# Two seams of a product stage: the place of its buffers, the last store of spectra and the first loads after it

## The chip, the cores and the metric

The kernel runs on one core of one Trainium2 chip as one launch. The metric is the device time of a run in microseconds (us). A run of the kernel is also recorded by the hardware profiler once; that execution has a time of its own and a span, from its first to its last instruction.

## The reference

Input is an image batch `x` of 16 x 128 channels x 32 x 32 (float32). Two layers follow, each with a mixing part and a token part, both with a residual. Cut to what matters:

```python
# layer 0
x = x + _L0_conv_ref(_ln_c(x), ...)        # linear attention
t = _to_tokens(x)                          # (16, 1024, 128)
t = t + _L0_ffn_ref(_ln_t(t), ...)         # spectral filters, see below
x = _from_tokens(t, x)
# layer 1
x = x + _L1_conv_ref(_ln_c(x), ...)        # two 3x3 convolutions
t = _to_tokens(x)
t = t + _L1_ffn_ref(_ln_t(t), ...)         # experts that choose tokens
x = _from_tokens(t, x)
```

The spectral part convolves every token sequence with 16 filters `phi`, once as it is and once with alternating signs, and multiplies the results with matrices `M_phi_plus` and `M_phi_minus`:

```python
U_plus = irfft(Vf[None, :, :, None] * Uf_p[:, :, None, :], n=n, axis=1)[:, :sl]
out = einsum('btkd,k,kde->bte', U_plus, s, Mpp) + einsum('btkd,k,kde->bte', U_minus, s, Mpm)
```

In the frequency domain this is one 128 x 128 complex matrix for each frequency, multiplied with the spectra of all 16 samples.

## The kernel before

The kernel has three stages, one after the other.

**Stage A** (to about 387 us) goes over the 16 samples in a software pipeline: attention, normalisation, and at last the spectrum `xf` of each sample. A dictionary of steps, `period`, gives the order. The last steps of a sample are `taps_add` (L633: a sum on VectorE, and the store of the sample to DRAM, `xd`, L634) and `odd_turns4` (L614: the last butterflies on POOL, and the store of the sample's spectrum to DRAM, `vd`, L615, 1 MB). `vd` has 16 chunks of frequencies as its first dimension. `prepare` stores weights for later (`wid`, L722).

**The product stage** (to about 664 us) goes over the 16 chunks `c`.
- `begin(c)` loads the chunk's spectra of all samples in four parts of four samples (`xc`, L778, issued on SP), and POOL makes sums and differences of each part (two L781 and one L782 each) into the tile `v`.
- `generate(c, q)` lets TensorE build a chunk's matrices from filters and `M_phi` (L790) in PSUM; `collect` copies them into the matrix buffer `g` (L801 on VectorE, L803 on ScalarE). There are two buffers `g`, for even and odd chunks, and the matrices of chunk `c + 1` are made between the products of chunk `c`.
- `multiply(c, m, x, ...)` makes the products of group `m` of four (L814). ScalarE copies them out of PSUM into one tile `yt` (L875), `combine` adds and subtracts its halves into the result tile `ys` (L842, L843, VectorE), and after the fourth group `finish` does four more sums (L828 to L831; on POOL, and on VectorE for the last chunk) and stores the results to DRAM, `yd`, in two parts (L835). `yd` consists of one tensor for chunks 0 to 13 and one for chunks 14 and 15.

TensorE's order at the start is: `generate` of chunk 0, eight more tiles of `generate` of chunk 1, then the first products.

**The last stage** loads, for each sample `b`, its tokens (`xt[b]` from `xd`, L974) and results (`yts[b]` from the two tensors of `yd`, L977), transforms back (`even`, `odd_sd`, `inverse`; L990 on POOL, L1003 on VectorE, L1074 on TensorE), adds (L1081), and goes through convolutions and experts. `planned` computes the order of its steps from fixed costs and due times; `load` is called for samples 0 and 1 ahead of all steps, for the others in the order. There are two buffers `y`, so the third sample's load waits for the first sample's back transform. In `load`, sample 0's tokens and the large parts of the results of samples 0 and 1 are issued on POOL, the rest on SP.

**Order and memory.** In a block with `manual_schedule` the named engines keep the order in which the program is written; instructions of different blocks can be mixed. SP is among the named engines in the last stage only. Each tile pool takes a stretch of every partition's memory, one after the other in the order of opening. A pool opened where others were closed reuses their bytes, and its first accesses wait for all accesses to every pool that lies under it, not only for the tiles under them: in the program, the first L781 waits for the last stores of `xd`, `vd` and `wid`. Addresses in bytes of a partition:

| Pools | Stage A | Product stage | Last stage |
|---|---|---|---|
| constants, weights | 18,976 to 68,640 | lower part as before | 18,784 to 95,232 (`wi`, `cw`, convolution tiles, two `y`) |
| working tiles | 68,640 to 167,552 | | 160,768 to 227,936 |
| `spool`: two `xf` | 167,552 to 183,936 | | |
| `xpool`: eight `x` | 183,936 to 216,704 | | 95,232 to 99,328 (`x0`), 99,328 to 160,768 (`x1` to `x15`) |
| `ppool`: staging of `prepare` | 216,704 to 227,456 | | |
| `gpl0`, `gpl1`: even and odd `g` | | 43,552 to 109,088, 109,088 to 174,624 | |
| `cpl`: two `v`, two `ys`, `yt`, `ye` | | 174,624 to 219,680 | |
| `xcl`: four `xc` | | 219,680 to 227,872 | |

Of the kernel before, what the change touches and what calls it, by code (L numbers as in the profile page):

```python
# [8 lines left out]
F32 = mybir.dt.float32  # L9
# [60 lines left out]
def metaformer_kernel(ctx: ExitStack, tc: tile.TileContext, io: dict, out: bass.AP):  # L70
# [96 lines left out]
    with ExitStack() as l0:  # L167
# [43 lines left out]
        with ExitStack() as a0:  # L211
# [132 lines left out]
            class Attention:  # L344
# [267 lines left out]

                def odd_turns4(self):
                    butterflies(self.ao, self.xf, 1, self.sd)  # L614
                    nc.sync.dma_start(  # L615
                        vd[:, :, self.b, :].rearrange("c p w -> p c w"),
                        self.xf.rearrange("p c x r m j -> p c (x r m j)"),
                    )

                def taps(self):  # L620

# [138 lines left out]


        with ExitStack() as g0:
            gpl = [g0.enter_context(tc.tile_pool(name=f"gpl{i}", bufs=1)) for i in range(2)]
            cpl = g0.enter_context(tc.tile_pool(name="cpl", bufs=2))
            xcl = g0.enter_context(tc.tile_pool(name="xcl", bufs=1))
            psg = g0.enter_context(tc.tile_pool(name="psg", bufs=8, space=PSUM))
            gs, vs = {}, {}
# [71 lines left out]

            def combine(c, m, ys, t):  # L840

                nc.vector.tensor_tensor(ys[:, :, 0, m], t[:, 1], t[:, 0], ALU.add)  # L842
                nc.vector.scalar_tensor_tensor(  # L843
                    ys[:, :, 1, m], t[:, 1], -1.0, t[:, 0], ALU.mult, ALU.add
                )
                if m == NM - 1:
                    finish(c, ys)

            with tc.manual_schedule(engines=PINNED):
# [5 lines left out]
                for c in range(NCH):  # L855
                    if c + 1 < NCH:
                        gs[c + 1] = gpl[(c + 1) % 2].tile([P, CW, C], F32, name="g", tag="g")

                    ys = cpl.tile([P, JL // RG, 2, NM, C], F32, name="ys", tag="ys")
                    for m in range(NM):  # L860
                        if c + 1 < NCH:
                            pg = [generate(c + 1, 2 * m + x) for x in range(2)]
                            collect(c + 1, 2 * m, pg[0])
                        if waiting:
                            combine(*waiting)
                        if c + 1 < NCH:
                            if m == 0:
                                begin(c + 1)
                            collect(c + 1, 2 * m + 1, pg[1])
                        py = psg.tile([P, 2, JL // RG, C], F32, name="py", tag="p")  # L870
                        fresh = set()
                        for x in range(2):
                            multiply(c, m, x, py, fresh)
                        t = cpl.tile([P, 2, JL // RG, C], F32, name="yt", tag="yt", bufs=1)
                        nc.scalar.copy(t, py)  # L875
                        waiting = c, m, ys, t
                combine(*waiting)


# [11 lines left out]
    with ExitStack() as c1:  # L891

        cconst = c1.enter_context(tc.tile_pool(name="cconst", bufs=1))
        first = c1.enter_context(tc.tile_pool(name="cfirst", bufs=1))
        xpool = [c1.enter_context(tc.tile_pool(name=f"xpool{i}", bufs=1)) for i in (2, 3)]
        work = c1.enter_context(tc.tile_pool(name="cwork", bufs=2))
        cps = c1.enter_context(ExitStack())
        ps = cps.enter_context(tc.tile_pool(name="cps", bufs=2, space=PSUM))
# [71 lines left out]
        yts = {}  # L970

        def load(b):
            xt[b] = xpool[b > 0].tile([P, N], F32, name=f"x{b}", tag=f"x{b}")
            (nc.sync if b else nc.gpsimd).dma_start(xt[b], xd[b])  # L974
            yts[b] = first.tile([P, 2, 2 * NM, C], F32, name="y", tag="y", bufs=2)
            for i, js in enumerate((slice(P - 2 * JL), slice(P - 2 * JL, P))):
                (nc.gpsimd if b < 2 and i == 0 else nc.sync).dma_start(  # L977
                    yts[b][js].rearrange("p r x e -> p r (x e)"),
                    yd[i][:, :, b].rearrange("j r x e -> j r (x e)"),
                )  # L980
# [758 lines left out]
```

## Time and profile before

| | |
|---|---|
| Runs | median 1273.64 us of three (1272.99 to 1274.5) |
| Profiled execution | 1271.01 us, span 1269.2 us |
| Busy, share of the span | PE 1149.1 us (91%), VectorE (DVE) 936.2 (74%), ScalarE (ACT) 725.9 (57%), POOL 605.3 (48%) |
| Mean granted TensorE clock | 0.967 of full speed |
| DRAM traffic | 164.64 MB, mean 130 GB/s |

The page cuts the span into 40 slices, and a digit is the busy share of one in tenths. The timeline has one row for a run of like instructions: start, duration, engine, line, operation, what is written and read, how many, and in brackets how long the engine was idle ahead of it and what ended that. SPq and POOLq are the engines' own queues, where loads and stores are issued; "to landing" is the time from there until the data is in place. A matmul of float32 gives two records. A chain of waits follows the work that ended last back from step to step.

### The profile page before, as it was taken

How to read it: one execution, taken by the hardware profiler on the slowest of the kernel's cores; microseconds unless marked ns; L12 is line 12 of the kernel's file. 1: busy time of each engine (PE TensorE's matmuls, PEld its weight loads, DVE VectorE, ACT ScalarE, POOL GpSimd, SP SyncE). 2: the span in 40 equal slices, each digit the busy share in tenths (PEclk: the TensorE clock that was granted, in tenths of full speed). 3: DMA queues.
4: the chain of work that ended last, by engine and by line, in shares of the span. 5: the costliest groups of instructions: out<-in, count | busy, mean ns of one | idle time of the engine just before them, and what ended most of it. 6: DMA issues, size and time to landing. Idle time of an engine off the chain costs nothing. (4 is left out here: it accounts for less than half of the span.)

```text
span 1269.2 us, 34025 instructions
## 1 busy us (share of the span) xinstructions
PE 1149.1 (91%) x14244; PEld 934.4 (74%) x14244; DVE 936.2 (74%) x1944; ACT 725.9 (57%) x1420; POOL 605.3 (48%) x801
## 2 busy tenths in 40 slices
PE   4889999999997999999976999999999999977975
PEld 3677777777776998888865888888898888853432
DVE  5788888888765777776765798889898888772325
ACT  4777777767654777777742354565565556542111
POOL 2335545565666688888863444333353442210002
PEclk9999999999998999999998999999999999985998
DMA  7105343443345244444458231213222212055976
GB/s 264 33 30 165 117 139 124 134 158 111 106 134 183 87 136 137 137 136 136 130 196 244 72 81 34 83 34 84 67 55 77 70 50 101 27 190 190 389 285 265
DMA packets 88346, 164.64 MB, mean 130 GB/s; under 512 B 5632, under 2 KB 41728, under 8 KB 87552
## 3 DMA queue, kind: packets, MB, share of 16 engines
q1 hardware_dynamic: 87312, 159.05, 38.6%
q0 software_dynamic: 880, 3.41, 0.8%
q8 instruction: 112, 1.84, 0.6%
q14 instruction: 42, 0.34, 0.1%
HBM read 105.03 MB, written 57.41 MB: 128 GB/s over the span
## 5 line engine op out<-in xcount | busy, mean ns | idle before, releaser
L958 PE MATMUL pcv<-v,cw 128*128 128x256 f32 x1152 | 259.7, 381 | 0.7 <-POOL v L1144 0.7
L958 PEld LDWEIGHTS pcv<-v,cw 128*128 128x128 f32 x1152 | 215.9, 191 | 34.3 <-issue 4.9
L801 DVE COPY g<-pg 128x512 f32<-128x512 f32 x196 | 127.8, 682 | 77.1 <-PE pg L790 77.1
L803 ACT COPY g<-pg 128x512 f32<-128x512 f32 x316 | 161.2, 605 | 31.7 <-PE pg L790 30.9
L790 PE MATMUL pg<-ph,mst 32*128 32x128 f32 x4096 | 139.6, 278 | 5.0 <-issue 3.5
L790 PEld LDWEIGHTS pg<-ph,mst 32*128 32x128 f32 x4096 | 126.0, 186 | 19.1 <-issue 12.4
L814 PE MATMUL py<-g,v 128*32 128x128 f32 x4096 | 127.9, 276 | 8.5 <-POOL v L781 5.7
L814 PEld LDWEIGHTS py<-g,v 128*32 128x32 f32 x4096 | 110.1, 111 | 18.3 <-POOL v L781 5.8
L144 ACT ACTIVATE tok<-tok,sts 128x128 f32<-128x128 f32 x256 | 101.9, 480 | 16.8 <-DVE sts L1031 13.4
L135 DVE BATCH_NORM_STATS2 bst<-big 128x6 f32<-128x256 f32 x256 | 91.1, 416 | 23.3 <-PE big L152 14.1
L781 POOL TENSOR_TENSOR v<-xc 128x256 f32<-128x256 f32 x128 | 99.8, 803 | 8.9 <-DMA xd<-x 8.9
L626 PE MATMUL big<-u,mu 128*128 128x128 f32 (+4 forms) x384 | 86.0, 380 | 0.0
L1144 POOL TENSOR_TENSOR v<-abss 128x256 f32<-128x256 f32 x64 | 49.1, 788 | 66.1 <-DVE abss L1140 54.3
L277 POOL TENSOR_TENSOR xf<-ab 128x256 f32<-128x256 f32 x34 | 24.8, 729 | 112.3 <-DVE ab L244 112.3
L1163 POOL TENSOR_TENSOR yo<-abss 128x256 f32<-128x256 f32 x32 | 23.5, 736 | 109.1 <-DVE abss L1159 109.1
L626 PEld LDWEIGHTS big<-u,mu 128*128 128x128 f32 x384 | 56.7, 191 | 18.0 <-issue 15.4
L875 ACT COPY yt<-py 128x512 f32<-128x512 f32 x64 | 37.5, 586 | 48.9 <-PE py L814 26.4
L1580 POOL TENSOR_TENSOR x<-yt,x 128x1024 f32<-128x1024 f32 x4 | 9.4, 2359 | 115.2 <-ACT yt L1579 115.2
L559 PE MATMUL big<-wf,ub 128*128 128x256 f32 x256 | 62.0, 385 | 0.2
L144 ACT ACTIVATE tt<-tt,sts 128x128 f32<-128x128 f32 x128 | 51.1, 481 | 14.6 <-DVE sts L1031 14.6
L152 PEld LDWEIGHTS big<-ident,x 128*128 128x128 f32 x384 | 46.0, 146 | 17.7 <-issue 10.5
L782 POOL TENSOR_SCALAR v<-v 128x256 f32<-128x256 f32 x64 | 55.2, 862 | 5.6
(247 smaller groups left out, 2480.5 us busy)
## 6 DMA issues: line engine op xcount, KB each, us to landing
we<-in_weight SPq DMA_DIRECT2D x32, 1024.0 KB, 9.9
vd<-xf SPq DMA_DIRECT2D x16, 1024.0 KB, 5.1
xc<-vd SPq DMA_DIRECT2D x64, 256.0 KB, 3.2
yd<-ys SPq DMA_DIRECT2D x32, 512.0 KB, 4.0
y<-yd SPq DMA_DIRECT2D x14, 896.0 KB, 6.7
x<-in_x SPq DMA_DIRECT2D x16, 512.0 KB, 4.6
mi<-in_M_phi SPq DMA_DIRECT2D x16, 512.0 KB, 4.7
xd<-x SPq DMA_DIRECT2D x16, 512.0 KB, 6.1
```

The source lines that it names most:

```text
L135: nc.vector.bn_stats(bst[:, j : j + 2, :].rearrange("p j s -> p (j s)"), src[:, j : j + 2, :].rearrange("p j c -> p c j"),)
L144: nc.scalar.activation(dst[:, j, :], src[:, j, :], AF.Identity, bias=nm[:, j : j + 1], scale=r[:, j : j + 1],)
L559: nc.tensor.matmul(dst, self.ub[:, q, :], wf[:, q, :], start=True, stop=True)
L626: nc.tensor.matmul(self.pa[:, a:hi], mu[:, NF - 1 - si, tap, :], self.u[:, a - tap : hi - tap], start=(tap == 0), stop=(tap == KU - 1),)
L781: nc.gpsimd.tensor_tensor(vv[:, x, 1:, bs], e, o, op)
L782: nc.gpsimd.tensor_scalar(v[:, :, 0, bs], v[:, :, 2, bs], -1.0, None, ALU.mult)
L790: nc.tensor.matmul(pg[r][:, i], mst[rs, 4 * q + i, :], ph[rs, c, :], start=True, stop=True,)
L801: nc.vector.tensor_copy(dst, src)
L803: nc.scalar.copy(dst, src)
L814: nc.tensor.matmul(py[rows, x, kl, :], v[:, (x * NM + m) * JL + jl, 1 - ri : 3 - ri, :] .rearrange("p k b -> p (k b)"), g[:, ((x * 2 + ri) ...
L958: nc.tensor.matmul(pc[:, i], wt[:, dy, k, :], v[:, k, dy * WT : dy * WT + HT], start=(dy == 0), stop=(dy == 2),)
L1144: nc.gpsimd.tensor_tensor(v[:, k, WT : WT + HT], self.ab[:, 0], self.ab[:, 1], op)
```

## The change

- `cpl` is opened between the two matrix buffers. `v`, results and sums then lie at 109,088 to 154,144, the odd buffer at 154,144 to 219,680; all else keeps its place.
- The spectrum of the last sample is stored in two pieces: chunk 0 (64 KB), then the other fifteen.
- For the last chunk, ScalarE copies only the first half of the products, into two halves of `yt` in turn, and VectorE reads the second half from PSUM.
- `x0` lies in one pool with the other samples, 95,232 to 160,768.
- The large part of sample 1's results is loaded from SP's queue, in its place in the program (after `x1`), not from POOL's.

```diff
                 def odd_turns4(self):
                     butterflies(self.ao, self.xf, 1, self.sd)
-                    nc.sync.dma_start(
-                        vd[:, :, self.b, :].rearrange("c p w -> p c w"),
-                        self.xf.rearrange("p c x r m j -> p c (x r m j)"),
-                    )
+                    for cs in (slice(0, 1), slice(1, NCH)) if self.b + 1 == B else (slice(NCH),):
+                        nc.sync.dma_start(
+                            vd[cs, :, self.b, :].rearrange("c p w -> p c w"),
+                            self.xf[:, cs].rearrange("p c x r m j -> p c (x r m j)"),
+                        )
...
-            gpl = [g0.enter_context(tc.tile_pool(name=f"gpl{i}", bufs=1)) for i in range(2)]
+            gpl = [g0.enter_context(tc.tile_pool(name="gpl0", bufs=1))]
             cpl = g0.enter_context(tc.tile_pool(name="cpl", bufs=2))
+            gpl.append(g0.enter_context(tc.tile_pool(name="gpl1", bufs=1)))
...
             def combine(c, m, ys, t):
-                nc.vector.tensor_tensor(ys[:, :, 0, m], t[:, 1], t[:, 0], ALU.add)
-                nc.vector.scalar_tensor_tensor(
-                    ys[:, :, 1, m], t[:, 1], -1.0, t[:, 0], ALU.mult, ALU.add
-                )
+                a, b = t
+                nc.vector.tensor_tensor(ys[:, :, 0, m], b, a, ALU.add)
+                nc.vector.scalar_tensor_tensor(ys[:, :, 1, m], b, -1.0, a, ALU.mult, ALU.add)
...
-                        t = cpl.tile([P, 2, JL // RG, C], F32, name="yt", tag="yt", bufs=1)
-                        nc.scalar.copy(t, py)
-                        waiting = c, m, ys, t
+                        if c + 1 < NCH or m == 0:
+                            t = cpl.tile([P, 2, JL // RG, C], F32, name="yt", tag="yt", bufs=1)
+                        if c + 1 < NCH:
+                            nc.scalar.copy(t, py)
+                            waiting = c, m, ys, (t[:, 0], t[:, 1])
+                        else:
+                            nc.scalar.copy(t[:, m % 2], py[:, 0])
+                            waiting = c, m, ys, (t[:, m % 2], py[:, 1])
...
-        xpool = [c1.enter_context(tc.tile_pool(name=f"xpool{i}", bufs=1)) for i in (2, 3)]
+        xpool = c1.enter_context(tc.tile_pool(name="xpool2", bufs=1))
...
         def load(b):
-            xt[b] = xpool[b > 0].tile([P, N], F32, name=f"x{b}", tag=f"x{b}")
+            xt[b] = xpool.tile([P, N], F32, name=f"x{b}", tag=f"x{b}")
             (nc.sync if b else nc.gpsimd).dma_start(xt[b], xd[b])
             yts[b] = first.tile([P, 2, 2 * NM, C], F32, name="y", tag="y", bufs=2)
             for i, js in enumerate((slice(P - 2 * JL), slice(P - 2 * JL, P))):
-                (nc.gpsimd if b < 2 and i == 0 else nc.sync).dma_start(
+                (nc.gpsimd if b + i == 0 else nc.sync).dma_start(
```

## The prediction

> **What bounds the kernel now.** I read the 40 slices first. TensorE is 90% busy or more nearly everywhere, so an engine is not what this change is about: the two places where it is not busy beside the product stage are.
>
> ```profile
> span 1269.2 us, 34025 instructions
> PE   4889999999997999999976999999999999977975
> ```
>
> The slice is 31.7 us. The 7 is the start of the product stage (381 to 412 us), the "76" its end (635 to 698). Then the busy time by stretches of 40 us around both:
>
> ```profile
> 400.00:440.00 40.00, 35.01 (x1065) 31.33 (x1069) 22.40 (x40) 24.48 (x48) 29.14 (x36) 0.91 0.35 101
> 440.00:480.00 40.00, 39.73 (x1287) 36.22 (x1279) 30.42 (x50) 31.15 (x61) 35.07 (x42) 1.00 0.42 137
> 640.00:680.00 40.00, 22.72 (x608) 21.04 (x600) 21.81 (x37) 10.73 (x21) 20.74 (x27) 0.79 0.67 234
> ```
>
> Second column: PE's busy us. Within the stage PE works 38 to 40 of 40 us, so a shift of its start moves its end by as much. The end loses 17 us. The timeline shows the **first seam**:
>
> ```profile
> 387.61 3.82 SPq L634 DMA_DIRECT2D xd<-x  x1
> 394.53 19.76 SPq L778 DMA_DIRECT2D xc<-vd  x9
> 396.00 1.43 POOL L781 TENSOR_TENSOR v<-xc 128x256 f32<-128x256 f32 x2 [8.89 <-DMA xd<-x]
> 405.39 2.76 PEld L814 LDWEIGHTS py<-g,v 128*32 128x32 f32 x56 [1.42 <-POOL v L782]
> 405.39 3.18 PE L814 MATMUL py<-g,v 128*32 128x128 f32 x56 [0.96 <-POOL v L782]
> ```
>
> POOL is idle 8.89 us, until the last `xd` store has landed (issued 387.61, 8.1 us to landing: 395.7). It has no use for that store: `v` lies where stage A kept `x` and `xf`, and a pool waits for all that lay under it. Then four passes of 2.33 us make `v` (396.00 to 405.34), and PE, done with `generate` at 398.11, waits for the last one. The fourth `xc` load stands behind the whole last `vd` store (387.14, 7.4 us, 394.5).
>
> The **second seam**:
>
> ```profile
> 653.07 2.07 DVE L842 TENSOR_TENSOR ys<-yt 128x256 f32<-128x256 f32 x1 [1.87 <-POOL ye L828]
> 655.06 2.17 DVE L843 SCALAR_TENSOR_TENSOR ys<-yt 128x256 f32<-128x256 f32 x1
> 656.88 0.71 POOL L977 DMA_DIRECT2D y<-yd  x1
> 657.34 0.59 ACT L875 COPY yt<-py 128x512 f32<-128x512 f32 x1 [4.36 <-DVE ys L843]
> 660.32 0.59 ACT L875 COPY yt<-py 128x512 f32<-128x512 f32 x1 [0.90 <-DVE ys L843]
> 663.40 0.42 DVE L831 TENSOR_TENSOR ys<-ye 128x256 f32<-128x256 f32 x1
> 670.33 0.64 SPq L977 DMA_DIRECT2D y<-yd  x1
> 673.79 2.04 PE L1074 MATMUL big<-wi,y 128*128 128x128 f32 x8 [16.27 <-DMA y<-yd]
> ```
>
> PE ends its products at 657.52. By then only one of the last four sums is made: the single `yt` makes copy and sums take turns, 1.48 us a turn. The last result is ready at 663.8, its stores land at 670.3 (5.3 and 6.1 us, beside 1.8 MB that POOL's two `y` loads fetch), the small `y` load takes 3.2, and PE starts after 16.27 us idle. The chain of waits then runs through the third `y`:
>
> ```profile
> 678.19 13.57 DMA y<-yd
> ```
>
> [...] L842 takes 0.41 us at least and 2.07 beside POOL's L829; L244, with one input in PSUM, stays within 674 to 693 ns in all 34 uses. [...] At 8 to 11 us, with POOL's and SP's queues both full, it shows 89 and 95 packets; at 657 to 663 us 364 and 138, so half is not sure. [...] Here the 56 matmul records after the 5.65 us pause take 3.18 us, 64 later ones 1.96.
>
> **The change, part by part.**
>
> *`v` below the odd matrix buffer, first chunk's spectra stored first.* The new place of the `cpl` pool (109,088 to 154,144) lies under stage A's working tiles alone, whose last user is POOL itself (387.1). So POOL waits only for its first `xc` (issued 385.61, 3.2 us: 388.8). Passes: 388.9, 391.2, 393.6, done 395.9. The fourth needs its `xc` load. SP's queue is then: store of chunk 0 (64 KB), store of the rest (one more issue, 0.4 us), `xd` (3.82 us of issuing, as the queue is full), then the load at about 391.9. It no longer waits for the landing at 394.5, but stands behind the same bytes; I put its landing 0.7 us after `xd`'s, 396.5. Fourth pass 396.5 to 398.85; PE starts the bulk of the first products at 398.95 instead of 405.39: 6.4 us. PE has then been idle for under 1 us, so the clock is not halved: 56 records at 1.96/64 are 1.7 us, not 3.18: 1.4 more. Sum **-7.8**. Ends: -8.7 if the load is early (PE is busy with `generate` to 398.11 in any case); -5.4 if it lands as late as now (397.55) and the clock is slow all the same. What is late next: the odd buffer now lies over `xf`, `x` and the staging tiles, so ACT's first copy into it, at 396.4, waits for `xd` (395.7). Cover 0.7 us; if `xd` slips by the extra issue of 0.4, still nothing; a slip beyond it moves PE one for one. POOL's passes now lie beside the copies of `generate`; in the stage they take 680 ns beside POOL and 677 without: nothing. Queued behind POOL's earlier work are only the next chunk's passes, not due for 16 us.
>
> *Last chunk.* ACT copies 256 columns: from 586 ns for 512 and 1013 for 1024 columns, about 0.37 each, and two alternating buffers free it from VectorE. The sums read one input from PSUM: 0.42 each, clear of POOL. Each of the four groups takes PE 1.75 us and VectorE under 1, so only the last is left at PE's end: copy to +0.4, sums to about +1.2, VectorE's four finishing steps (2.2) to +3.4, against +6.3 now: **2.9** earlier.
>
> *Second `y` on SP; `x0` in the common pool.* POOL's second `y` load (0.9 MB) goes behind the last stores, and `x0` too: the `x` pool now lies over `v` and results, so its first load waits for the last `yd` store. Also, POOL's finish of chunk 14 loses three issues (0.61, 0.72, 0.71), so its stores go out about 1.2 us earlier. The last pair of stores then has the engines to itself: the pair at 640.7 landed 4.5 us after its first issue, so +3.45+4.5 = +7.95, against +12.8 now: another 1.9 us, 4.8 in all. The small load then lands at +11.2 against +16.0.
>
> Against it: POOL issues in order, `x0` **ahead of the first large `y`** (L974, then L977). That `y` is here at 663.5 now, long before it is needed; it will be issued at about +8.7. Both together are 1.44 MB, the SP queue beside them (small `y`, `x1`, second `y`) 1.6 MB. Data starts 1.2 us after the issue (+9.4); at half of some 420 GB/s the POOL queue needs 6.9 us: +16, with 1 us to landing **+17**. PE starts at about +17.2 instead of +16.3: the 4.8 us are spent, and 0.9 more. Bounds: +14.5 with the share of 657 to 663 us; +20.5 if it takes the 11.1 us of the second `y` now.
>
> The third `y`, which ends the next wait, is bound by bytes. Before it, 2.3 MB more have to pass after the results (5.5 us at 420 GB/s), starting 4.6 us earlier; but the queue is empty for 2 us (669.5 to 671.5) now. From the state of the queue when PE starts, it lands between 2 us earlier and 1.5 later, and VectorE waits 3.2 us for it now (691.85), so up to that can show. Second seam in all: **-0.4**, range -3 to +4.
>
> *Free of charge:* SP's extra issue, and `x1` to `x15`, whose pool waited for the last product already. Nothing else in the last stage moves: its tiles keep their addresses and its order is fixed.
>
> Sum: -7.8 - 0.4 = -8.2 against the profiled execution's 1271.0 (span 1269.2 and 1.8 around it): 1262.8. That execution lies 2.6 below the median of the runs, 1273.64; to that I apply the difference: **1265.5**.
>
> **Rivals.**
> 1. *The second seam gives more.* The third `y` lands 2 us early and POOL's queue gets its larger share: -3 there, 1262.5. For it: 364 against 138 packets. Against: those stores had come later into the queue.
> 2. *A new wait at the first seam.* The fourth load lands as late as now, or the odd buffer's wait on `xd` shows: -5.4 to -6.8, about 1267.5. For it: only 0.7 us of cover. This is also the case in which the split store does nothing.
> 3. *POOL's queue costs 3 to 6 us.* The first `y` lands at +20 to +22: 1269 to 1272, about no change at the worst. For it: loads behind a full queue took 11 to 14 us at this very place.
> 4. *Slower.* The same mechanism at its worst: `x0` goes first (5.5 us), and `y`'s data then comes at the 13.5 us of the third `y`: +8.05+5.5+13.5 = +27, PE 11 us late, net +3: 1277. It decides from a landing later than +24, some 15 us after the issue. Against: today's two loads overlap (issued 1.9 us apart, landed 5.1 apart, the larger one 8.7 us after its issue).
>
> **Chances.** Likeliest 0.52; rival 1 0.15; 2 0.11; 3 0.16 (half of it beyond the bound of no change); 4 0.06. About 0.2% (2.5 us) is what a measurement of this kernel can tell from none. Faster: 0.52+0.15+0.11+0.10 = 0.88; within 0.05; slower 0.07. The range goes from rival 1 with an early load (1261) into rival 3 (1271).
>
> **What would show it.** Right: POOL's first L781 near 388.9, PE's first full products near 399 at 31 ns a record; last results 3.4 us after PE's end, their stores landed by +8; POOL issuing `x0` then, and PE's first L1074 about 17 us after its end, waiting for POOL's `y` and not SP's. Wrong: L781 still at 396; PE idle at the first seam over 2 us; PE idle over 24 us at the second.

## The result, and the profile after

The changed kernel takes 1269.74 us (median of 20 runs) where the kernel before, run beside it, takes 1277.28 us (median of 20): a ratio of 0.9947, with a 95% interval of 0.9928 to 0.9966. That is 6.8 us less, with an interval of 4.3 to 9.2. (The ratio is not the quotient of the two medians, which lie 7.5 us apart.) Measured once more later, the ratio was 0.9950 (0.9932 to 0.9969). The kernel before against itself gave 1.0002 (0.9982 to 1.0023). The profiled execution of the changed kernel took 1270.07 us, with a span of 1268.3 us.

That span is only 0.9 us below the one of before. One profile against one other does not show this gain, because the executions differ by several us in places that the change does not touch: the first matmul of `generate` starts at 386.0 us in one execution of the kernel before and at 393.8 in another, and from the first copy into `yt` to the last product the two take 248.9 and 250.8 us (254.7 in a third kernel with the same layout, 253.3 and 254.8 in the changed one). So I compare the two seams by times counted from a point close by: the **first seam** from the first matmul of `generate` ("gen": 385.99 before, 387.79 after), the **second seam** from the end of the last product ("end": 657.52 before, 659.01 after).

The page after, its first line and PE's slices:

```profile
span 1268.3 us, 34024 instructions
PE   4889999999998999999974999999999999977975
```

The thirteenth digit, the slice of the stage's start, was a 7 and is an 8; at the stage's end "76" has become "74". The timeline of the changed kernel at the first seam (its line numbers are a few higher than those of the kernel before: L783 was L781, L816 was L814):

```profile
387.79 12.12 PE L792 MATMUL pg<-ph,mst 32*128 32x128 f32 x320 [1.41 <-DVE x L634]
388.90 0.80 SPq L616 DMA_DIRECT2D vd<-xf  x2
389.80 3.82 SPq L635 DMA_DIRECT2D xd<-x  x1
390.87 1.43 POOL L783 TENSOR_TENSOR v<-xc 128x256 f32<-128x256 f32 x2 [2.00 <-ACT g L805]
394.08 14.90 SPq L780 DMA_DIRECT2D xc<-vd  x8
400.04 1.43 POOL L783 TENSOR_TENSOR v<-xc 128x256 f32<-128x256 f32 x2 [2.14 <-DMA xc<-vd]
402.45 3.22 PE L816 MATMUL py<-g,v 128*32 128x128 f32 x56 [1.20 <-POOL v L784]
```

POOL begins at gen +3.1 instead of +10.0; its wait for `xd` is gone. Three passes later it has a new wait of 2.14 us, for the fourth `xc` load. That load is issued at 394.08, as soon as the small piece of the spectra has landed (394.02), takes 5.9 us and lands at 399.97, gen +12.2; before it was at +11.6. TensorE begins the bulk of its first products at +14.7 instead of +19.4, and 56 records still take 3.22 us: as before, the granted clock is half (0.50 from 402.36 to 405.76; 64 later records, at 1.00, take 1.95 us).

The timeline of the changed kernel at the second seam and at the third sample of the last stage:

```profile
659.11 0.37 ACT L881 COPY yt<-py 128x256 f32<-128x256 f32 x1 [1.38 <-PE py L816]
659.51 0.42 DVE L845 TENSOR_TENSOR ys<-py,yt 128x256 f32<-128x256 f32 x1 [0.99 <-ACT yt L881]
661.97 0.42 DVE L833 TENSOR_TENSOR ys<-ye 128x256 f32<-128x256 f32 x1
666.40 0.64 SPq L983 DMA_DIRECT2D y<-yd  x1
667.09 0.62 POOL L980 DMA_DIRECT2D x<-xd  x1 [12.41 <-DMA yd<-ys]
667.70 0.69 POOL L983 DMA_DIRECT2D y<-yd  x1
678.89 2.04 PE L1080 MATMUL big<-wi,y 128*128 128x128 f32 x8 [19.89 <-DMA y<-yd]
682.37 1.24 SPq L983 DMA_DIRECT2D y<-yd  x2
692.37 0.73 POOL L996 TENSOR_TENSOR z<-y 128x256 f32<-128x256 f32 x1 [3.05 <-PE big L1080]
693.41 0.66 DVE L1009 TENSOR_TENSOR z<-y 128x256 f32<-128x256 f32 x1
```

The results are ready at end +3.4 (before +6.3), their stores have landed by +7.3 (before +12.8). POOL, whose sums are long done, waits 12.41 us for those stores, issues `x0`, and 0.6 us later the first large `y`, which lands at 678.69, +19.7. TensorE idles 19.89 us, 3.6 more than before.

The last two rows show where this lateness ends. In the kernel before, the same place reads:

```profile
677.55 1.23 SPq L977 DMA_DIRECT2D y<-yd  x2
691.85 0.42 DVE L1003 TENSOR_TENSOR z<-y 128x256 f32<-128x256 f32 x1 [3.16 <-DMA y<-yd]
691.92 0.94 POOL L990 TENSOR_TENSOR z<-y 128x256 f32<-128x256 f32 x1 [7.40 <-DMA y<-yd]
```

There VectorE and POOL wait for the third `y`, to +34.3 and +34.4. Afterwards they take the third sample up at +34.4 and +33.4 and wait for no `y`: POOL was kept by TensorE, which was late (its own 3.05 us of waiting end with L1080). The first `y`'s lateness has eaten up the wait for the third one. The adds (L1087, before L1081) of the first six samples come at +22.6, 29.9, 51.0, 72.7, 100.5, 128.0 before and at +25.9, 33.3, 53.4, 75.0, 102.6, 128.4 after.

### The profile page after: what moved, and what is told of

It reads as the page before. It is cut to its first block, busy times and chain, and to the rows that moved or that the text cites. A ratio compares the mean times of both kernels' runs of the same rounds, so it can differ in the third digit from the quotient of the medians.

```text
span 1268.3 us, 34024 instructions
## 1 busy us (share of the span) xinstructions
PE 1141.3 (90%) x14244; PEld 931.8 (73%) x14244; DVE 931.4 (73%) x1944; ACT 725.0 (57%) x1420; POOL 603.7 (48%) x800
## 5 line engine op out<-in xcount | busy, mean ns | idle before, releaser
L805 ACT COPY g<-pg 128x512 f32<-128x512 f32 x316 | 161.2, 606 | 31.9 <-PE pg L792 31.2
L792 PEld LDWEIGHTS pg<-ph,mst 32*128 32x128 f32 x4096 | 126.9, 186 | 20.5 <-issue 13.5
L816 PE MATMUL py<-g,v 128*32 128x128 f32 x4096 | 126.8, 276 | 6.3 <-issue 1.9
L816 PEld LDWEIGHTS py<-g,v 128*32 128x32 f32 x4096 | 109.6, 111 | 16.3 <-issue 3.9
L135 DVE BATCH_NORM_STATS2 bst<-big 128x6 f32<-128x256 f32 x256 | 91.1, 416 | 22.1 <-PE big L152 12.3
L783 POOL TENSOR_TENSOR v<-xc 128x256 f32<-128x256 f32 x128 | 98.7, 794 | 4.1 <-DMA xc<-vd 2.1
L144 ACT ACTIVATE tt<-tt,sts 128x128 f32<-128x128 f32 x128 | 51.1, 481 | 14.9 <-DVE sts L1037 14.9
L152 PE MATMUL big<-ident,x 128*128 128x128 f32 x384 | 52.2, 281 | 6.6 <-DVE x L1225 4.8
L464 POOL TENSOR_TENSOR ke<-ke,ks 128x1024 f32<-128x1024 f32 x16 | 30.6, 1913 | 57.2 <-DVE qs L472 45.6
## 6 DMA issues: line engine op xcount, KB each, us to landing
we<-in_weight SPq DMA_DIRECT2D x32, 1024.0 KB, 11.2
```

The lines of the kernel that those rows point to most:

```text
L135: nc.vector.bn_stats(bst[:, j : j + 2, :].rearrange("p j s -> p (j s)"), src[:, j : j + 2, :].rearrange("p j c -> p c j"),)
L144: nc.scalar.activation(dst[:, j, :], src[:, j, :], AF.Identity, bias=nm[:, j : j + 1], scale=r[:, j : j + 1],)
L152: nc.tensor.transpose(pt[:, j, :], src[:, j * P : (j + 1) * P], ident)
L783: nc.gpsimd.tensor_tensor(vv[:, x, 1:, bs], e, o, op)
L792: nc.tensor.matmul(pg[r][:, i], mst[rs, 4 * q + i, :], ph[rs, c, :], start=True, stop=True,)
L805: nc.scalar.copy(dst, src)
```

## The experiments

The table is read from the traces: first sum of POOL, landing of the fourth `xc` load and bulk of the products (ninth product record) in us from gen; idle time of TensorE, landing of the third `y` and add of the sixth sample in us from end. Each ratio is to the kernel before on the same chip, with its 95% interval.

| Kernel | Ratio | POOL | 4th load | Bulk | PE idle | Third y | 6th add |
|---|---|---|---|---|---|---|---|
| before | 1 | 10.0 | 11.6 | 19.4 | 16.3 | 34.2 | 128.0 |
| before, again (e12) | 1.0002 (0.9982–1.0023) | 10.7 | 12.4 | 20.1 | 13.9 | 31.2 | 124.9 |
| after | 0.9947 (0.9928–0.9966) | 3.1 | 12.2 | 14.7 | 19.9 | 32.5 | 128.4 |
| after, again (e6) | 0.9950 (0.9932–0.9969) | 3.0 | 11.9 | 14.4 | 21.3 | 36.8 | 130.7 |
| layout only (e1) | 0.9938 (0.9913–0.9963) | 2.9 | 11.8 | 14.3 | 15.3 | 33.7 | 125.5 |
| PSUM sums only (e7) | 0.9988 (0.9966–1.001) | 10.7 | 12.4 | 20.1 | 15.1 | 34.3 | 129.7 |
| x0 apart (e2) | 0.9911 (0.9887–0.9936) | 3.0 | 11.9 | 14.3 | 11.2 | 31.5 | 125.1 |
| y ahead of x0 (e8) | 0.9931 (0.9902–0.9959) | 3.0 | 11.3 | 13.8 | 10.9 | 33.8 | 127.2 |
| whole store (e3) | 0.9983 (0.9963–1.0002) | 3.0 | 11.8 | 14.3 | 20.8 | 35.4 | 129.8 |
| whole store, again (e11) | 0.9971 (0.9951–0.9991) | 3.3 | 12.4 | 14.9 | 20.0 | 33.0 | 128.5 |
| early parts (e4) | 0.9963 (0.9945–0.9981) | 0.1 | 9.1 | 12.9 | 19.9 | 33.2 | 129.2 |
| early parts, x0 apart (e5) | 0.9925 (0.9889–0.996) | 0.1 | 9.2 | 12.3 | 11.5 | 31.7 | 125.5 |
| stores on POOL (e9) | 0.9968 (0.9947–0.9989) | 3.3 | 12.1 | 14.6 | 20.9 | 34.4 | 129.5 |
| stores on POOL, x0 apart (e10) | 0.9941 (0.9922–0.996) | 3.3 | 12.4 | 14.9 | 12.4 | 32.1 | 125.6 |

### One part of the change alone (e1, e7)

e1 is the kernel before with `cpl` opened between the two matrix buffers, and nothing else:

```diff
-            gpl = [g0.enter_context(tc.tile_pool(name=f"gpl{i}", bufs=1)) for i in range(2)]
+            gpl = [g0.enter_context(tc.tile_pool(name="gpl0", bufs=1))]
             cpl = g0.enter_context(tc.tile_pool(name="cpl", bufs=2))
+            gpl.append(g0.enter_context(tc.tile_pool(name="gpl1", bufs=1)))
```

> The kernel before with one edit, the cpl pool between the two matrix buffers; the store of spectra stays whole, the sample pools, the loads and the last chunk stay as they were. Times below are counted from the first generate matmul of the product stage. Theory A (POOL's wait for x and xf was all that the first seam held): POOL's first sum starts at +3 instead of +10, the fourth xc load lands at +11.6 as in the kernel before because it waits for the whole store, PE begins the bulk of its first products at about +14 instead of +19.4. 5 us less in all, about 0.4%. Theory B (the split of the store carries part of it): PE begins later here than in the changed kernel (+14.7), by as much as the whole store is slower. At the second seam as before: PE idle for 16.3 us.

The timeline of e1 (its first matmul of `generate` starts at 388.21):

```profile
391.15 1.43 POOL L782 TENSOR_TENSOR v<-xc 128x256 f32<-128x256 f32 x2 [1.85 <-ACT g L804]
400.10 1.43 POOL L782 TENSOR_TENSOR v<-xc 128x256 f32<-128x256 f32 x2 [1.91 <-DMA xc<-vd]
402.52 3.09 PE L815 MATMUL py<-g,v 128*32 128x128 f32 x56 [1.20 <-POOL v L783]
```

Measured: 0.9938, so the layout alone gives as much as the whole change; the other four edits together give nothing that can be told from zero. Its first seam is that of the changed kernel (POOL at +2.9, bulk at +14.3), although the last spectra are stored whole. Of the four, the sums are tested alone (e7), and the split store and the common pool of `x0` are taken back (e3, e2); the move of sample 1's results to SP's queue is in no run taken back alone.

e7 is the kernel before with the sums of the last chunk from PSUM alone:

```diff
-                        t = cpl.tile([P, 2, JL // RG, C], F32, name="yt", tag="yt", bufs=1)
-                        nc.scalar.copy(t, py)
-                        waiting = c, m, ys, t
+                        ...
+                            nc.scalar.copy(t[:, m % 2], py[:, 0])
+                            waiting = c, m, ys, (t[:, m % 2], py[:, 1])
```

> The kernel before, with one part of the change alone: for the last chunk ScalarE copies 256 columns into two halves of yt in turn and VectorE sums from PSUM. Layout, store, x0 and both y loads as before. Theory (the sums are made sooner, but the loads of y fetched beside the last stores are unchanged): results ready 3.4 us after TensorE's end (before 6.3), the small y lands 2.5 to 3 us earlier than +16.0, TensorE idles 13 to 14 us instead of 16.3; first add 2.5 us earlier, that of the sixth sample by 0.5 to 1 only; ratio 0.998 to 1.000. Rival (the start of the last stage sets the end, one for one): 2.9 us, ratio 0.9975 or less, and the later adds earlier by as much.

The timeline of e7 (its last product ends at 669.57):

```profile
668.45 0.71 POOL L981 DMA_DIRECT2D y<-yd  x1
672.52 0.42 DVE L831 TENSOR_TENSOR ys<-ye 128x256 f32<-128x256 f32 x1
681.27 0.64 SPq L981 DMA_DIRECT2D y<-yd  x1
684.70 2.05 PE L1078 MATMUL big<-wi,y 128*128 128x128 f32 x8 [15.13 <-DMA y<-yd]
```

Results are ready at +3.4, as in the changed kernel. The three executions with the old copies have them at +6.3 (before), +5.5 (e1) and +5.0 (e12), so 1.6 to 2.9 us of this gain are real. But POOL's two large loads of `y` still go out ahead of the last stores (in the kernel before packets of POOL's queue ran to 667.4, with the last stores issued at 663.8 and 664.2), the small `y` is issued at +11.7, and TensorE idles 15.1 us, between the two executions of before (16.3 and 13.9). In time it is no gain that can be told from none: 0.9988, with 1 inside the interval.

### x0 and the first large y (e2, e8)

e2 is the changed kernel with the second pool of `x` back, so that the pool of `x0` no longer lies over the memory of the results:

```diff
-        xpool = c1.enter_context(tc.tile_pool(name="xpool2", bufs=1))
+        xpool = [c1.enter_context(tc.tile_pool(name=f"xpool{i}", bufs=1)) for i in (2, 3)]
...
-            xt[b] = xpool.tile([P, N], F32, name=f"x{b}", tag=f"x{b}")
+            xt[b] = xpool[b > 0].tile([P, N], F32, name=f"x{b}", tag=f"x{b}")
```

> The changed kernel with x0 in a pool of its own again, so that POOL can load x0 and the first large y during the last chunk. Theory A (x0's wait ahead of y in POOL's queue makes the second seam long): PE idle between the last product and the first back transform falls from 19.9 to 11 to 13 us, and the whole run gets 3 to 8 us shorter than the changed kernel. Theory B (a late start of the last stage is absorbed there, since the third y and the order by hand set the pace of the first samples): the idle time falls as much, the addition of the sixth sample stays within 1 us of where it is in the changed kernel counted from the last product (128.4 us), and the whole differs by under 2 us.

The timeline of e2 (its last product ends at 655.46):

```profile
649.18 0.62 POOL L980 DMA_DIRECT2D x<-xd  x1
651.05 0.71 POOL L983 DMA_DIRECT2D y<-yd  x1
666.66 2.04 PE L1080 MATMUL big<-wi,y 128*128 128x128 f32 x8 [11.20 <-DMA y<-yd]
687.07 0.43 DVE L1009 TENSOR_TENSOR z<-y 128x256 f32<-128x256 f32 x1 [5.18 <-DMA y<-yd]
```

`x0` and the first large `y` are issued while the products still run (the `y` lands at 658.02, +2.6), and TensorE waits for the small `y` alone. The idle time falls by 8.7 us against the changed kernel, but the sixth add comes only 3.3 us earlier, and VectorE now waits 5.18 us for the third `y`. Ratio 0.9911: the lowest of this study, 3.6 thousandths below the changed kernel (0.9947), though the two intervals still touch.

e8 is the changed kernel with the common pool kept, and the order of the two loads on POOL turned round:

```diff
-            xt[b] = xpool.tile([P, N], F32, name=f"x{b}", tag=f"x{b}")
-            (nc.sync if b else nc.gpsimd).dma_start(xt[b], xd[b])
+            if b:
+                xt[b] = xpool.tile([P, N], F32, name=f"x{b}", tag=f"x{b}")
+                nc.sync.dma_start(xt[b], xd[b])
...
+            if b == 0:
+                xt[b] = xpool.tile([P, N], F32, name=f"x{b}", tag=f"x{b}")
+                nc.gpsimd.dma_start(xt[b], xd[b])
```

> The changed kernel with one order turned round: POOL issues the first large y ahead of x0, so y waits for the last-stage buffers of its own only and not behind x0, which waits for the last results store. Theory (x0 ahead of y in POOL's queue is what makes y late): y is issued before TensorE's products end and lands before the small y does, TensorE starts 11 to 12 us after its last product, as with x0 apart (11.2), and since x0 is needed only for the first add, that add is 1 to 4 us later than with x0 apart; ratio 0.991 to 0.993. Rival (the bytes in the queues make y late, not the order): TensorE idles 17 us or more.

The timeline of e8 (its last product ends at 656.31):

```profile
649.98 0.76 POOL L984 DMA_DIRECT2D y<-yd  x1
664.41 0.60 POOL L990 DMA_DIRECT2D x<-xd  x1 [10.87 <-DMA yd<-ys]
667.16 2.05 PE L1084 MATMUL big<-wi,y 128*128 128x128 f32 x8 [10.85 <-DMA y<-yd]
```

The large `y` goes out at -6.3 instead of +8.7, and TensorE idles 10.85 us. So the late `y` of the changed kernel is a matter of order: POOL issues in program order, `x0` stands first, and the pool it lies in is free only when the last results are stored. The first add is not late either (+16.9; with x0 apart +17.7). `x0` itself still loads after the last stores here, and the third `y`, issued at +17.4 as with x0 apart (+17.6), lands 2.3 us later (+33.8 against +31.5).

### The fourth load at the first seam (e3, e11, e4, e9)

e3 and e11 are the changed kernel with the last spectra stored whole:

```diff
-                    for cs in (slice(0, 1), slice(1, NCH)) if self.b + 1 == B else (slice(NCH),):
-                        ...
+                    nc.sync.dma_start(
+                        vd[:, :, self.b, :].rearrange("c p w -> p c w"),
```

> The changed kernel with the last sample's spectra stored in one piece again. Theory A (the split brings nothing, because the small piece lands only 5.1 us after its issue, behind the three xc loads, and the fourth load then stands behind the rest of the store and xd): fourth load lands at +11.6 from the first generate matmul (changed kernel: +12.2), PE's bulk of first products at about +14 (+14.7), whole within 1 us of the changed kernel. Theory B (the split is what moved the fourth load): it lands later than +12.2, and the whole gets 1 to 3 us longer.

> The changed kernel with the last sample's spectra stored whole, once more and unaltered: its first time was 0.36% above the changed kernel's, though its first seam was the same within 0.4 us. Theory (the split does nothing, the difference was spread between executions): ratio 0.994 to 0.997, bulk of products at +14 to +15, fourth load issued when the whole store has landed and landed at +11.5 to +12.2. Rival (the split is worth 0.3%): ratio 0.998 or more again.

With the whole store the fourth load of e3 is issued at gen +8.1, 1.8 us later than in the changed kernel (+6.3), but takes 3.7 us instead of 5.9 and lands at +11.8; in e11 3.4 us, at +12.4. The bulk begins at +14.3 and +14.9 (changed kernel +14.7 and +14.4). In the profile, then, the split does nothing: the load issued 1.8 us earlier takes 2.2 us longer. In the changed kernel it goes out with both stores under way: the last packets of 512 bytes (spectra) and of 4096 (`xd`) start at 396.30 and 397.41, and the first of the loads issued from 394.08 on (2048 bytes) at 395.70. The times do not say so as plainly: 0.9983 and 0.9971 are both above 0.9947 and 0.9950, by about 0.3% in the mean. But the intervals of e11 and e6 overlap, and by the plain medians e11 (1271.30 of 1276.82, 0.9957) lies no higher than e6 (1271.95 of 1276.99, 0.9961). No place at the two seams answers to the difference. It stays open.

e4 is the changed kernel with `prepare` advanced twice at one sample, so that its last store (`wid`), whose staging tiles the `xc` buffers reuse, is out of the way earlier:

```diff
-                    next(preparing, None)
+                    for _ in range(2 if p == 8 else 1):
+                        next(preparing, None)
```

> The changed kernel with one step of the weight staging taken one period of stage A earlier, so that the store of wid, for which the xc tiles wait, has landed long before; the first three xc loads then go out before the last spectra are stored. Theory A (the small piece and the fourth load are late because of the bytes of the first three loads ahead of them): the small piece lands 3 us after its issue instead of 5.1, the fourth load at about +8 to +9 from the first generate matmul instead of +12.2, PE starts the bulk of its products at +12.3 to +13 without a pause of over 1 us and at full clock (56 records in 1.8 us instead of 3.2); 3 to 4 us less than the changed kernel. Theory B (the fourth load stands behind the rest of the store and xd in SP's queue whatever went before): it lands within 1 us of now, and the whole within 1 us.

The timeline of e4:

```profile
389.06 12.26 PE L793 MATMUL pg<-ph,mst 32*128 32x128 f32 x320 [1.41 <-DVE x L634]
389.07 0.80 SPq L616 DMA_DIRECT2D vd<-xf  x2
391.38 10.91 SPq L781 DMA_DIRECT2D xc<-vd  x6
401.81 1.95 PE L817 MATMUL py<-g,v 128*32 128x128 f32 x61 [0.15 <-issue]
```

With the first three `xc` loads gone before it, the small piece lands 1.6 us after its issue (5.1 in the changed kernel), the fourth load is issued at +2.3 and lands at +9.1. TensorE passes the seam without a wait, at the full clock (granted 1.00 from 394 to 408): 61 records in 1.95 us. This is the start and the clock that the prediction had put at the first seam, though not by its path alone: POOL begins 2.8 us earlier too (+0.1), and TensorE is busy with `generate` to +12.3. In time it brought nothing that can be told from none: 0.9963 (changed kernel 0.9947 and 0.9950), and with x0 apart 0.9925 (e5) against 0.9911 without. Whether stage A, which now does this work elsewhere, pays it back, the profiles cannot tell: gen lies at 389.06 here and at 387.8 and 387.5 in the changed kernel, but that is well inside the 8 us between two executions of the kernel before.

> Both changes that helped one seam each, on top of the changed kernel: prepare advanced twice at p == 8 (staging stores and their tiles out of the way earlier), and x0 again in a pool of its own, so that POOL issues x0 and the first large y while the products still run. Theory (the seams add up): at the first seam the fourth spectra load lands about 9 us after the first generate matmul and TensorE starts its bulk of products at about +12.9 (changed kernel +14.7) with an unslowed clock, at the second it idles 11 to 12 us (changed kernel 19.9); time 5 to 8 us below the changed kernel's, ratio to before 0.988 to 0.991. Rival (the last stage has its own limit from the sixth sample on, and what is won at the first seam is lost in the spread between executions): ratio as with x0 apart alone, 0.991 to 0.993.

e9 moves the bytes that are issued ahead of the fourth load to another queue (e10 does the same with x0 apart):

```diff
-                        nc.sync.dma_start(
+                        (nc.gpsimd if cs.start == 1 else nc.sync).dma_start(
...
+                    if self.b + 1 == B:
+                        nc.gpsimd.dma_start(xd[self.b], self.x)
```

> The changed kernel, and for the last sample the large piece of the spectra (0.94 MB) and the store of the sample, xd (0.5 MB), are issued on POOL after its last butterflies instead of on SP; the piece with chunk 0 stays on SP. Theory (the fourth spectra load is late because it stands behind these bytes in SP's queue: its 5.9 us from issue to landing are 3 us of a free load and 3 us of queue): with the bytes in another queue it is issued at +5.5 to +6.5 from the first generate matmul as before or a little sooner, takes 3 to 4.5 us, lands at +9.5 to +10.5 instead of +12.2, TensorE starts the bulk of the products at +12.4 to +13.2 instead of +14.4 to +14.7, with an unslowed clock. First seam 1.5 to 2.5 us better than the changed kernel; ratio 0.992 to 0.995. Rival (the load shares the DMA engines with the same bytes whichever queue they are in): lands after +11.5, bulk at +14 or later. Rival of the other side: POOL's issues, or the odd buffer's wait for these stores, delay POOL's first sum of v beyond +4 or the first copies into the odd buffer: seam no better.

> The kernel with both stores of the last sample on POOL, and x0 again in a pool of its own. Theory (the two seams are independent): first seam as with the stores on POOL alone (bulk at +12.4 to +13.2), TensorE idle 11 to 12 us at the second seam, third y landed 31 to 32 us after the last product; ratio 0.988 to 0.991. Rival (x0 apart is all that counts): ratio 0.991 to 0.993 and the bulk at +14 or later.

The load takes 6.7 us (397.13 to 403.82) and lands at +12.1, no earlier than with all in one queue. The transfers of e9 by queue, in the stretches 397 to 398.5, 398.5 to 400 and 400 to 401.5 us (packets, MB, share of the 16 engines; q0 is POOL's, q1 SP's):

```profile
q0 software_dynamic: 118, 0.47, 100.7%
...
q0 software_dynamic: 115, 0.42, 97.7%
...
q1 hardware_dynamic: 140, 0.26, 78.8%
q0 software_dynamic: 47, 0.13, 33.9%
```

For 3 us POOL's stores hold all 16 engines and SP's load, issued at 397.13, moves nothing; its first packet goes at 400.23. Not all of that is waiting: the fourth load of the kernel before, with only the end of the `xd` store ahead of it, moved its first packet 1.0 us after its issue (394.53, 395.49). So 2.1 of the 3.7 us by which this load takes longer (6.7 against 3.0) pass while POOL's stores hold the engines; the other 1.6 come after its first packet and are not placed. Why SP's queue had no turn in those 2.1 us is not shown. The second queue did not let the short load pass the long stores. Both kernels are no faster than those with the stores on SP (0.9968; 0.9941 against 0.9911 with x0 apart).

### The same kernels again (e6, e12)

> The changed kernel once more, unaltered, beside the other three on one chip: what two measurements of one kernel differ by. Theory (spread of the executions only): ratio 0.993 to 0.997; seams as in its first profile within 1 us (bulk of products +14 to +15 us from the first generate matmul, 19 to 21 us idle before the back transform), the length of the product stage anywhere between 250 and 254 us. Rival (the changed layout makes the product stage some 3 us longer): 253 us or more again, where the kernel before had 248.9.

> The kernel before, unaltered, against itself: how far ratio and seams of one kernel scatter. Theory: ratio 0.998 to 1.002; bulk of products at +19 to +20.5, TensorE idle 15 to 17 us at the second seam, sixth sample's add 126 to 130 us after the last product, product stage 249 to 255 us from its first copy. Rival (what is attributed to the changes lies in the order of measuring): ratio off 1 by more than 0.002.

The ratios repeat (0.9950, 1.0002). The product stage of the changed kernel took 253.3 and 254.8 us from its first copy, but e7, in the old layout, took 254.7: the new layout is not shown to lengthen the stage (all eleven executions of it: 250.1 to 254.8, mean 252.4; the three of the old: mean 251.5). Counted from gen to end, the stage is 266.5 to 271.6 us long in the new layout (mean 269.2) and 271.5 to 278.1 in the old (mean 274.6): what the first seam gains is still there when the products end. At the second seam one kernel scatters by 2 to 3 us: the sixth add of before lies at +128.0 and +124.9. The groups separate in part. The six executions with the order of the changed kernel (after, e3, e4, e6, e9, e11) give 128.4 to 130.7, mean 129.4; the three with x0 apart 125.1 to 125.6, mean 125.4; the four with the loads as before (before, e1, e7, e12) 124.9 to 129.7, mean 127.0. The first two groups lie apart; the third overlaps both.

## Why the prediction was right, and where it was not

The prediction was -8.2 us of 1273.6, a ratio of 0.9936; measured were 0.9947 and 0.9950, some 6.4 to 6.8 us. The direction and the mechanism of the first seam hold, and e1 puts the gain in the layout; several terms do not hold.

**First seam: -7.8 forecast (-6.4 for the start of the bulk, -1.4 for the clock); -4.7 in the first pair of profiles, -6.0 on average (-5.5 and -0.6).** (The start is a mean over the three executions of the old layout, +19.8, and the seven of the new one without e4, e5, e9 and e10, +14.4; their 56 records take 3.2 and 2.6 us in the mean.) POOL's start was right but for 0.2 us: at 388.9 in the time of the kernel before, which is +2.9; +3.1 measured. POOL's four passes and the copies beside them cost what was said. Two terms failed.
- *"I put its landing 0.7 us after `xd`'s, 396.5."* That is +10.5; the load landed at +12.2, 2.05 us after `xd` (397.92). Of the 1.7 us, 0.35 are `xd` itself, which landed later than forecast, and 1.35 the distance behind it; the kernel before already had 1.8 us there (397.55 after 395.76). The sentence before it, that the load "stands behind the same bytes", fits the runs: issued later (e3, +11.8), or with the stores in another queue (e9, +12.1), it lands within 0.4 us of the same time. The three passes were done at 397.9, so 2.1 us of POOL's gain turned into the new wait. This was rival 2's first half; its landing "as late as now" (+11.6) was still 0.6 us too early.
- *"The clock is not halved: 1.4 more."* It was: 3.22 us for 56 records. TensorE pauses there for 0.92 and 1.20 us, not for under 1; together that is just over the 2 us that the prediction had named as a sign of being wrong. For one pause of under 1 us the profile of before bears the forecast out: there single pauses of 0.72 to 1.64 us at full clock (1.64 from 104.24) left it full. Of the seven executions of the new layout four ran at half (after, e1, e3, e11), one for a part (e6, 2.35 us) and two not (e2 and e8, 1.74), and e3 with pauses of 0.53 and 1.20 us did where e2 with 0.60 and 1.20 did not.

  The clock records of the traces show what went with it. In all fourteen the granted clock changed only on a grid of 3.41 us, the same through the whole execution (in the kernel before it was half for two steps from 401.58 and for five from 660.99). A stretch of that grid at full clock in which TensorE was busy (by the profile's records) for less than 40% was followed by half clock in 113 cases of 113, for more than 55% by full clock in 4614 of 4614, and between the two by half in 35 of 84; in the profiles of before and after alone the counts are 17 of 17, 659 of 659 and 3 of 13. The stretch with the pauses was busy for 41% in the changed kernel (1.40 us, from 398.94 to 402.35) and half clock followed; e8's was busy for 63% and full clock followed; of e2 and e3, both at 49%, full clock followed in e2 and half in e3. As far as these counts go, then, the term hung on where the pauses fall in the grid, which the prediction had not asked, and pauses of 1.7 to 2.4 us in sum were enough here.

e4 removes the late load and finds both terms as forecast (bulk at +12.9, forecast +13.0; full clock). The load was not in time in the changed kernel.

**Second seam: -0.4 forecast, with -3 to +4 (a middle between bounds; no sum of the prediction gives it).** In the first pair of profiles the sixth add is +0.4; over the groups +2.3. Step by step:
- *Results ready +3.4, last stores landed +7.95:* measured +3.4 and +7.3. The copies (0.37) and sums (0.42 and 0.41) were as worked out. Of the 1.8 MB that the prediction put beside the last stores, the first 0.9 had landed (+6.0) before these were issued (+6.3). That the stores of chunk 14 go out 1.2 us earlier is not shown: they went at -4.3 in the changed kernel and at -1.7 to -2.7 in e3, e4, e9 and e11, with the loads as before at -0.6 to -1.8. The -4.3 is in part a late end: TensorE pauses for 1.47 us within the last chunk (2.12 in e6), waiting for nothing that the profile shows.
- *"That `y` will be issued at about +8.7":* +8.69. *"+17":* it landed at +19.7, and at +21.1 in e6. Two terms are at fault, by about as much. The data of POOL's queue starts at +10.6, not at +9.4: 2.5 us after the issue of `x0` (in the kernel before 2.6; on SP's queue the fourth `xc` took 1.0 there and the small `y` 1.4). And it takes 8.0 us, not 6.9, because of the rate. I gave POOL's queue half of 420 GB/s, which the kernel before moves from 664 to 666 us. It had about half, but of less. The transfers of the changed kernel by queue from 673 to 675 us:

```profile
DMA packets 150, 0.61 MB, mean 307 GB/s; under 512 B 0, under 2 KB 0, under 8 KB 150
## 3 DMA queue, kind: packets, MB, share of 16 engines
q1 hardware_dynamic: 75, 0.31, 50.7%
q0 software_dynamic: 75, 0.31, 50.4%
```

From 669 to 677 us the means are 360, 365, 307 and 317 GB/s, 337 in all, and POOL's queue moved 1.44 MB of 2.69. The profile of before had two figures for two busy queues, 429 GB/s at 8 to 11 us and 315 at 657 to 663; the second, from the place itself, was the one to take. This is rival 3's mechanism (+20 to +22). Its price, 3 to 6 us, was too high, since it took the start of the last stage for its end.
- *Third `y` between 2 us earlier and 1.5 later.* It came 1.7 us earlier in the first profile (+32.5) and 2.5 later than before in e6 (+36.8). What I had not followed is the buffer: there are two, so the third `y` is issued when the first sample's transform has read its own. The late first `y` therefore delays the third one's issue (682.37 is +23.4; before +20.0), and only a shorter flight gives that back: 8.6 us against 13.5, but 11.5 in e6. That the queue is less full by then would explain it, and is not shown.

That 8.7 us of idle time are worth about 3 in e2 is the same cushion seen from the other side: without the late start, the third `y` is again what the last stage waits for.

**The sum.** The seams as averaged (-6.0 and +2.3) make -3.7; the times say -6.4 to -6.8, with 4.0 at the least. Nor does e4's gain in its profile reappear in its time. A third place, which no seam holds and the prediction had not looked at, makes the executions differ. The granted clock in the pages of before, after and e6:

```profile
PEclk9999999999998999999998999999999999985998
PEclk8999999999999999999997999999999999997998
PEclk7999999999999999999987999999999999985998
```

The fourth digit from the right, the slice from about 1142 to 1174 us, is a 5 in six of the fourteen executions (before, e12, e3, e4, e5, e6) and a 7 in the other eight. From the sixth add to the end the six take 483.7 to 484.8 us, the eight 478.2 to 481.8: some 4 us. They part at one stretch of the 3.41-us grid: at half clock TensorE was busy there for 84 to 99% in the eight (86% from 1156.70 in the changed kernel), and full clock followed; for 75 to 82% in the six (75% from 1155.92 in the kernel before), and half clock lasted for four stretches more. Why is not shown: within those four a stretch busy for 100% was followed by half clock too (before, from 1159.34). Both executions of the kernel before are of the long kind, one of the two of the changed kernel. Over all recorded runs the mean granted clock is 0.967 for the changed kernel and 0.961 to 0.963 for the kernel before, and within one kernel a run with 0.001 more is 0.5 to 0.9 us shorter. The shorter stretch at half clock at the first seam (6.8 to 10.2 us in the old layout, 3.4 or none in the new) is 0.001 to 0.004 of that difference of 0.005. So part of the measured gain goes with the clock, and perhaps not all of that part with the seams; whether the change makes the long kind rarer, or chance did, no run shows. That is open.

**The rivals.** Rival 1 (second seam gives 3 more) did not happen. Rival 2 happened in its first half: the load was late, and with it the split store did nothing; the odd buffer's wait on `xd` did not show. Rival 3 happened in mechanism and not in price; half of its chance of 0.16 is 0.08, and the sum for "faster" had 0.10. Rival 4, a `y` later than +24, did not: the latest landed at +21.1.

## What to carry to other kernels

A buffer's place decided which earlier transfers its first use waited for (POOL began at +2.9 in e1 instead of +10.0); moving it cost nothing here and alone gave as much as the whole change, so look at what lies under a buffer before tuning what is in it. The load that read what was just stored landed at +11.3 to +12.4 in all but two kernels: splitting the store moved its issue and not its landing, another queue for the stores did not move its landing either, and only taking other transfers out of its way did (+9.1 and +9.2). When an idle stretch shrinks or grows, look for the next wait along the same stage before counting it: 8.7 us of idle time were worth about 3 here at the sixth add, because a later load then set the pace. And before a small gain is put down to a change, look where else the executions differ: the clock in one late slice was worth some 4 us here.

## What the runs showed of the hardware that was not expected

- POOL's stores of 1.4 MB kept all 16 DMA engines (101% and 98% of their time) for 3 us in which another queue's load, already issued, moved no packet (e9); some 2 of them were waiting. With two long queues of loads in the changed kernel POOL's queue moved 148 packets to 52 in one stretch of 2 us (671 to 673) and 75 to 75 in the next.
- With both queues busy with such loads, 337 GB/s were moved (669 to 677 us), not the 420 that I had taken; at 8 to 11 us of the kernel before, also with both queues busy, it was 429, with packets of 7 KB in the mean instead of 4.
- The granted TensorE clock changed on a grid of 3.41 us in all fourteen executions, and a stretch at full clock that was busy for less than 40% was followed by half clock in 113 cases of 113, one busy for more than 55% in none of 4614: pauses of 1.73 us in sum, with eight product records between them, halved it in one execution (e3), and pauses of 1.80 us did not in another (e2).
